# A transformer block on one NeuronCore: where the first group's mean and scale copy, and its first two q/k evictions, stand in the order of ScalarE and VectorE

## The chip, the core and the metric

The kernel runs on 1 core of one Trainium2 chip, as one launch. The metric is the device time of that core in microseconds (us); lower is better. All data are fp32 in memory. A large operand of a matmul is held as two parts, a rounded high part and the rest (`hi` and `lo`), and a product takes three matmuls (`hi*hi`, `hi*lo`, `lo*hi`) or, for some, two.

## The reference, cut to what matters

```python
x = x + _layernorm(attn(_layernorm(x), Wqkv, bqkv, Wo, bo))     # x: 1 x 2048 x 1024, head width d = 256
x = x + _layernorm(ffn(_layernorm(x), W_gate, W_up, W_down))    # F = 2752
# attn:
qkv = einsum('bsc,cf->bsf', x, Wqkv) + bqkv          # q, k, v: 2048 x 256 each
attn = softmax(einsum('bqd,bkd->bqk', q, k) / sqrt(d))
out = einsum('bqk,bkd->bqd', attn, v) @ Wo + bo
# ffn: silu(x @ W_gate.T) * (x @ W_up.T) @ W_down.T
```

The change lies in the first stage, the q, k and v of the normalised `x`. The kernel multiplies the raw `x` by the weights and puts the layer norm in afterwards: with the row mean m and the row scale r, (x - m) r W = r (x W - m sum(W)), so that each result needs m, r and the sums of the weights' columns when it leaves the accumulator bank.

## The kernel before, in words

**Tiles.** The 2048 rows are four groups (g = 0 to 3) of 512, each of four blocks (tb) of 128. PSUM has eight banks of 128 x 512 fp32. `bank[0]` to `bank[3]` take the four q/k results of a group (two halves of k, two of q, features on the partitions); `vb[0]` to `vb[3]` (banks 6, 7, 4, 5) take the four v blocks (rows on the partitions). The fp32 staging tiles (`f4`, `f2p`, `stage`, 4 KB a partition each) are used again and again, for columns of x, rows of x and weights.

**The steps of a group.**
- `x_parts` (L183 on ScalarE, L184 on VectorE) makes the high and the low part of the group's columns of x.
- `row_stats` (VectorE, L196 to L199) or `row_stats_scalar` (ScalarE L204 and L206, GpSimd L205 and L207 to L209) finds m and r of a block of rows.
- `store_mr` and `load_mr` (SP) write a group's m and r to memory and read them back broadcast over the partitions; `turn_mr` (L220, ScalarE) copies them into the order in which q/k need them.
- `qk` (L127 to L129, TensorE, 24 matmuls into one bank) and `v_block` (L245 and L246, 16 matmuls into one bank) do the products. In the first group the products of v are made by `v_part` instead, before q and k.
- `qk_out` evicts a q/k bank: L231 (VectorE) reads the bank, the means from `turn_mr`'s copy and one column of the weight sums `nws`; L232 (VectorE) multiplies by r; L235 (ScalarE) adds the bias and rounds to the high part; L236 (VectorE) makes the low part. After L231 the bank is free.
- `v_out` evicts a v bank: L250, L252 (not in the first group) and L253 on VectorE, the copy L254 on ScalarE, the rest L255 on VectorE. The staging `vst` has two halves, so block tb + 2 overwrites that of tb.
- `take_sum(i)` (L387, ScalarE) sums one fourth of the rows of the turned q/k weights `wqk_t`, loaded by `load_sum`, into column i of `nws`.

**Order.** In this stage nearly every operation is kept in the order in which the program text names it (`pin`), on each engine by itself; an engine works through its own list in order and waits on semaphores for the others. So the order of the text is the order of each engine's list. The DMAs of this stage are all issued by SP, in text order too. From the end of the stage on, the main loop over 16 blocks of scores (`scores`, `softmax`, `turn`, `attend`, `proj`) and then the feed-forward part are placed by a scheduler; only some of their operations are pinned.

The text around the change, before: after the fourth q/k product of group 0 come the four evictions of group 0's v blocks, each followed by one weight sum; then `turn_mr(0)`; then four loads; then the first two v blocks of group 1 with their evictions; then the q/k evictions of group 0, with the row statistics of group 1's last two blocks between them. TensorE's list at that place is: the four `qk(0, i)`, the four `v_block(1, tb)`, the four `qk(1, i)` into the same banks 0 to 3, the four `v_block(2, tb)`, and so on.

Of the kernel before, what the change touches and what calls it, by code (L numbers as in the profile page):

```python
# [24 lines left out]
TB = G // P  # L25
# [9 lines left out]
def block_kernel(ctx, tc, x, xt, wqk, wqk_t, wv, bqk, bv, wo, bo, wgu, wlast, wd, out):  # L35
# [17 lines left out]
    def tl(p, shape, dt, name):  # L53
        return p.tile(shape, dt, tag=name, name=name, bufs=1)
# [17 lines left out]
    def small_tile():  # L72
        small_n[0] += 1
        return small[small_n[0] % NSM]

    bank_pool = pool("banks", space=PSUM)
    bank = [tl(bank_pool, [P, 512], F32, f"bank{i}") for i in range(8)]
# [28 lines left out]
    def f32(ap):  # L106
        return ap.bitcast(F32)
# [27 lines left out]
    def kT(d, g):  # L135
        return slot(kx, 4 * d + g)
# [3 lines left out]
    def vt(k, h=slice(0, 2)):  # L140
        return (a1 if k < 8 else late_v[0]).rearrange("p a b c -> p (a b c)").rearrange("p (k h d) -> p k h d", h=2, d=D)[:, k % 8, h, :]
# [27 lines left out]
    def load(dst, src):  # L169
        pin(nc.sync.dma_start(dst, src))  # L170
# [5 lines left out]
    def load_row(g, tb):  # L176
        t = g * TB + tb
        load(row_room[g][tb], x[t * P : (t + 1) * P, :])

    def x_parts(g, c0, n, r):  # L180
        d = xT[g % 2][:, c0 : c0 + n, :, :]
        v = r[:, : n * G].rearrange("p (c t) -> p c t", c=n)
        pin(nc.scalar.copy(d[:, :, 0, :], v))  # L183
        pin(nc.vector.tensor_tensor(d[:, :, 1, :], v, f32(d[:, :, 0, :]), ALU.subtract))  # L184

    def m_of(g, tb):
        return yg[g][:, 2 * tb : 2 * tb + 1]

    def r_of(g, tb):
        return yg[g][:, 2 * tb + 1 : 2 * tb + 2]  # L190
# [10 lines left out]
    def row_stats_scalar(g, tb):  # L201

        s, r = small_tile(), row_room[g][tb]
        pin(nc.scalar.activation(r, r, AF.Identity, accum_out=s[:, 0:1]))  # L204
        pin(nc.gpsimd.tensor_scalar(s[:, 1:2], s[:, 0:1], -1.0 / C, None, ALU.mult))  # L205
        pin(nc.scalar.activation(r, r, AF.Square, bias=s[:, 1:2], accum_out=s[:, 2:3]))  # L206
        pin(nc.gpsimd.tensor_scalar(m_of(g, tb), s[:, 0:1], 1.0 / C, None, ALU.mult))  # L207
        pin(nc.gpsimd.tensor_scalar(s[:, 3:4], s[:, 2:3], 1.0 / C, EPS, ALU.mult, ALU.add))
        pin(nc.gpsimd.tensor_tensor(r_of(g, tb), s[:, 3:4], mhalf, ALU.pow))  # L209
# [8 lines left out]
    def turn_mr(g):  # L218

        pin(nc.scalar.copy(  # L220
            mr[g].rearrange("q (k b p) -> q k b p", k=2, b=TB), mr_raw[g].rearrange("q (p b k) -> q k b p", k=2, b=TB)
        ))
# [6 lines left out]
    def qk_out(g, i, b, pin=pin):  # L229
        s, bias = qst[i % 2], bqk_s[:, i : i + 1]  # L230
        pin(nc.vector.scalar_tensor_tensor(s, mr[g][:, L], nws[:, i : i + 1], b, ALU.mult, ALU.add))  # L231
        pin(nc.vector.tensor_tensor(s, s, mr[g][:, R], ALU.mult))  # L232
        if i < 2 or g == 0:
            dst = kT(i, g) if i < 2 else qa[:, i - 2, :, :]
            pin(nc.scalar.activation(dst[:, 0, :], s, AF.Identity, bias=bias))  # L235
            pin(nc.vector.scalar_tensor_tensor(dst[:, 1, :], s, bias, f32(dst[:, 0, :]), ALU.add, ALU.subtract))  # L236
        else:
            pin(nc.scalar.activation(s, s, AF.Identity, bias=bias))
            pin(nc.sync.dma_start(q_d[g][:, i - 2, :], s))

    def v_block(g, tb, b, pin=pin):
        xg = xT[g % 2]
        cols = slice(tb * P, (tb + 1) * P)
        for c in range(8):
            pin(nc.tensor.matmul(b, xg[:, c, 0, cols], wv_s[:, c, :, :].rearrange("p a f -> p (a f)"), start=(c == 0), stop=False))  # L245
            pin(nc.tensor.matmul(b[:, D:], xg[:, c, 1, cols], wv_s[:, c, 0, :], start=False, stop=(c == 7)))  # L246

    def v_out(g, tb, b, both=True, pin=pin):
        k, s = g * TB + tb, vst[tb % 2]
        pin(nc.vector.scalar_tensor_tensor(s, nwv, m_of(g, tb), b[:, :D], ALU.mult, ALU.add))  # L250
        if both:
            pin(nc.vector.tensor_tensor(s, b[:, D:], s, ALU.add))  # L252
        pin(nc.vector.scalar_tensor_tensor(s, s, r_of(g, tb), bv_s, ALU.mult, ALU.add))  # L253
        pin(nc.scalar.copy(vt(k, 0), s))  # L254
        pin(nc.vector.tensor_tensor(vt(k, 1), s, f32(vt(k, 0)), ALU.subtract))  # L255
# [25 lines left out]
    def hi(dst, src):  # L281
        pin(nc.scalar.copy(dst, src))
# [20 lines left out]
    vb = bank[6], bank[7], bank[4], bank[5]  # L303
# [82 lines left out]
    def take_sum(i):  # L386
        pin(nc.scalar.activation(col_room[1][i], col_room[1][i], AF.Identity, scale=-1.0, accum_out=nws[:, i : i + 1]))  # L387
# [13 lines left out]
        row_stats_scalar(1, tb)  # L401
        load_row(2, tb + 2)
    hi(nwv, vb[0][:, D:])
    for tb in range(TB):
        v_out(0, tb, vb[tb], False)
        take_sum(tb)
    load(bo_s, bo.partition_broadcast(P))


# [93 lines left out]

    cols = lambda g, n: load_cols(g, 2 * n, 2, col_room[g][n])
    parts = lambda g: [x_parts(g, 2 * n, 2, col_room[g][n]) for n in range(4)]
    turn_mr(0)
    cols(2, 0)
    cols(2, 1)
    load_row(2, 0)
    load_row(2, 1)  # L510
    for tb in range(2):
        v_block(1, tb, vb[tb])
        v_out(1, tb, vb[tb])
    qk_out(0, 0, bank[0])
    row_stats_scalar(1, 2)
    qk_out(0, 1, bank[1])
    row_stats_scalar(1, 3)
    cols(2, 2)
    cols(2, 3)
# [854 lines left out]
```

## Time and profile before

| What | Value |
|---|---|
| Time, median of 3 runs | 1664.43 us (1662.71, 1664.43, 1665.21) |
| The profiled execution's own time | 1662.63 us |
| Its span, first to last instruction | 1660.8 us |
| Around the span | 1.8 us |
| TensorE matmul busy in the span | 1648.2 us (99%) |
| VectorE / ScalarE / GpSimd busy | 1105.0 / 736.4 / 107.5 us |
| Mean granted TensorE clock | 0.999 |

The profile is of one execution, and its times are counted from the start of the span. "PE" is TensorE's matmuls, "PEld" its weight loads, "DVE" VectorE, "ACT" ScalarE, "POOL" GpSimd, and "SPq" the queue in which SP issues DMAs. L231 is line 231 of the kernel before. A row of the timeline gives start, duration, engine, line, operation and tiles, and in square brackets the engine's idle time ahead of it with what ended it. Idle time of an engine that does not set the end costs nothing. The staging tile of the v evictions appears as `f`, that of the q/k evictions as `f2p`, the bank's second operand as `ys` (statistics and weight sums).

### The profile page before, as it was taken

The numbers are of one execution on the slowest core, as the hardware profiler recorded it, in microseconds if no ns is written. First come the engines' busy times: TensorE is split into PE (matmuls) and PEld (weight loads), VectorE is DVE, ScalarE is ACT, GpSimd is POOL, SyncE is SP. The second block draws the span as 40 slices with busy tenths as digits, with TensorE's granted clock in tenths as the row PEclk, the third lists the DMA queues.
The fourth block names the chain that finished last, engine by engine and source line by source line (L and its number), as shares of the span: only waits on it lengthen the run. The fifth ranks groups of instructions, "written<-read, shape, count | busy, mean of one in ns | idle before, by whom it ended". The sixth has DMA issues, their size and how long they took to land.

```text
span 1660.8 us, 21107 instructions
## 1 busy us (share of the span) xinstructions
PE 1648.2 (99%) x7705; PEld 1375.0 (83%) x7705; DVE 1105.0 (67%) x1657; ACT 736.4 (44%) x1094; POOL 107.5 (6%) x157
## 2 busy tenths in 40 slices
PE   9999999999999999999999999999999999999998
PEld 8788888888888888888888888888888888888887
DVE  6656677668877777777587458965556665455458
ACT  5673555445544444444365344433333333354342
POOL 3020000000011111111000001100000000000001
PEclk9999999999999999999999999999999999999999
DMA  8452133435756666656468656533222233676653
GB/s 316 156 185 70 46 107 107 139 121 191 232 182 215 220 215 227 205 198 216 143 228 276 196 190 222 187 134 105 101 96 95 96 102 121 229 261 197 197 186 123
DMA packets 137545, 283.62 MB, mean 171 GB/s; under 512 B 14304, under 2 KB 31072, under 8 KB 137440
## 3 DMA queue, kind: packets, MB, share of 16 engines
q1 hardware_dynamic: 136288, 280.30, 50.4%
q10 hardware_dynamic: 1152, 1.97, 0.3%
q8 instruction: 60, 0.98, 0.2%
q14 instruction: 45, 0.37, 0.1%
HBM read 198.31 MB, written 83.90 MB: 170 GB/s over the span
## 4 chain that ended last, share of the span: by engine, by line
PE 95%; DMA 2%; DVE 1%; ACT 1%; issue 0%; SPq 0%; POOL 0%; POOLq 0%; DVEq 0%
PE bank L859 73%; PE bank L127 4%; PE bank L128 4%; PE bank L129 4%; PE bank L460 3%; PE bank L444 2%; PE bank L461 2%; PE bank L245 1%; PE bank L592 1%; DMA stage<-wqk 1%; DMA f<-xt 0%; PE bank L246 0%; DMA stage<-wqk_t 0%; PE bank L1045 0%; PE bank L1044 0%
## 5 line engine op out<-in xcount | busy, mean ns | idle before, releaser
L859 PE MATMUL bank<-a 128*128 128x512 f32 (+1 forms) x960 | 226.4, 386 | 0.0
L859 PE MATMUL bank<-xb,a 128*128 128x512 f32 x912 | 212.2, 389 | 0.0
L859 PEld LDWEIGHTS bank<-a 128*128 128x128 f32 x960 | 179.1, 188 | 36.6
L859 PEld LDWEIGHTS bank<-xb,a 128*128 128x128 f32 x912 | 171.0, 188 | 35.4
L110 ACT CAST a<-f2p 128x1024 fp32r<-128x1024 f32 (+2 forms) x123 | 107.0, 870 | 113.4 <-PE bank L859 86.1
L111 DVE TENSOR_TENSOR a<-f2p,a 128x1024 fp32r<-128x1024 f32 (+2 forms) x123 | 122.3, 995 | 45.5 <-ACT a L110 41.6
L111 DVE TENSOR_TENSOR a<-f,a 128x1024 fp32r<-128x1024 f32 (+1 forms) x70 | 78.6, 1122 | 102.7 <-ACT a L110 98.6
L859 PE MATMUL bank<-kx,a 128*128 128x512 f32 x612 | 146.0, 389 | 0.0
L859 PEld LDWEIGHTS bank<-kx,a 128*128 128x128 f32 x612 | 114.9, 188 | 23.8
L859 PE MATMUL bank<-wvo 128*128 128x512 f32 (+1 forms) x498 | 120.9, 386 | 0.0
L873 DVE TENSOR_TENSOR p_s<-bank,p_s 128x512 f32<-128x512 f32 x96 | 65.1, 681 | 79.5 <-PE bank L859 43.8
L859 PEld LDWEIGHTS bank<-wvo 128*128 128x128 f32 x498 | 92.9, 188 | 18.9
L110 ACT CAST a<-f 128x1024 fp32r<-128x1024 f32 (+1 forms) x70 | 57.8, 825 | 103.0 <-PE bank L859 98.5
L859 PE MATMUL bank<-kx,wvo 128*128 128x512 f32 x420 | 100.1, 389 | 0.0
L859 PE MATMUL bank<-a,a 128*128 128x512 f32 x420 | 99.4, 389 | 0.0
L859 PEld LDWEIGHTS bank<-kx,wvo 128*128 128x128 f32 x420 | 78.8, 188 | 16.4
L859 PEld LDWEIGHTS bank<-a,a 128*128 128x128 f32 x420 | 78.8, 188 | 16.4
L111 DVE TENSOR_TENSOR wvo<-f,wvo 128x1024 fp32r<-128x1024 f32 (+1 forms) x47 | 54.6, 1162 | 49.2 <-ACT wvo L110 49.2
L859 PE MATMUL bank<-a1b,wvo 128*128 128x512 f32 x360 | 86.6, 389 | 0.0
L859 PEld LDWEIGHTS bank<-a1b,wvo 128*128 128x128 f32 x360 | 67.6, 188 | 14.0
L859 PE MATMUL bank<-kx 128*128 128x512 f32 (+1 forms) x339 | 78.5, 387 | 0.0
L859 PEld LDWEIGHTS bank<-kx 128*128 128x128 f32 x339 | 63.4, 188 | 13.0
(329 smaller groups left out, 3078.5 us busy)
## 6 DMA issues: line engine op xcount, KB each, us to landing
f2p<-wgu SPq DMA_DIRECT2D x41, 512.0 KB, 5.5
hd_S<-p_s SPq DMA_DIRECT2D x60, 256.0 KB, 4.6
f<-x SPq DMA_DIRECT2D x28, 512.0 KB, 4.2
f<-wgu SPq DMA_DIRECT2D x22, 512.0 KB, 3.5
wr<-wgu SPq DMA_DIRECT2D x21, 512.0 KB, 5.5
f<-wd SPq DMA_DIRECT2D x20, 512.0 KB, 5.3
hd_A<-xi SPq DMA_DIRECT2D x40, 256.0 KB, 2.0
td_T<-f SPq DMA_DIRECT2D x40, 256.0 KB, 4.5
```

The lines of the kernel that those rows point to most:

```text
L110: nc.scalar.copy(hi, src)
L111: (lo_engine or nc.vector).tensor_tensor(lo, src, f32(hi), ALU.subtract)
L127: pin(nc.tensor.matmul(o, w[0], m[0], start=first, stop=False))
L128: pin(nc.tensor.matmul(o, w[0], m[1], start=False, stop=False))
L129: return pin(nc.tensor.matmul(o, w[1], m[0], start=False, stop=last))
L245: pin(nc.tensor.matmul(b, xg[:, c, 0, cols], wv_s[:, c, :, :].rearrange("p a f -> p (a f)"), start=(c == 0), stop=False))
L444: nc.tensor.transpose(b[:, n * P : (n + 1) * P], p_s[:, k * P : (k + 1) * P], ident)
L460: nc.tensor.matmul(b, p[:, k, 0, :], vt(k).rearrange("p h d -> p (h d)"), start=(k == 0), stop=False)
L461: nc.tensor.matmul(b[:, D:], p[:, k, 1, :], vt(k, 0), start=False, stop=(k == NKB - 1))
L592: nc.tensor.transpose(o[:, j * P : (j + 1) * P], a[:, cb * P : (cb + 1) * P], ident)
L859: one = nc.tensor.matmul(o, w[i], m[j], start=first and n == 0, stop=last and n == 2, skip_group_check=chained)
L873: nc.vector.tensor_tensor(o, a, b, op)
```

## The change

Two things move, and no instruction is added or taken away. The copy `turn_mr(0)` goes from behind the four v evictions and weight sums of group 0 to a place behind the first v eviction; the weight sums come one eviction later in the text than they did. The first q/k eviction of group 0, `qk_out(0, 0)`, goes ahead of the first two v blocks of group 1, and the second one, with the row statistics before it, goes between those two blocks' evictions.

```diff
@@ end of the first group @@
     hi(nwv, vb[0][:, D:])
-    for tb in range(TB):
+    v_out(0, 0, vb[0], False)
+    turn_mr(0)
+    for tb in range(1, TB):
         v_out(0, tb, vb[tb], False)
-        take_sum(tb)
+        take_sum(tb - 1)
+    take_sum(TB - 1)
     load(bo_s, bo.partition_broadcast(P))
@@ start of the second group @@
-    turn_mr(0)
     cols(2, 0)
     cols(2, 1)
     load_row(2, 0)
     load_row(2, 1)
+    qk_out(0, 0, bank[0])
     for tb in range(2):
         v_block(1, tb, vb[tb])
         v_out(1, tb, vb[tb])
-    qk_out(0, 0, bank[0])
-    row_stats_scalar(1, 2)
-    qk_out(0, 1, bank[1])
+        if tb == 0:
+            row_stats_scalar(1, 2)
+            qk_out(0, 1, bank[1])
     row_stats_scalar(1, 3)
     cols(2, 2)
     cols(2, 3)
```

In the built program TensorE's and GpSimd's lists are the same as before. ScalarE's and VectorE's differ only in the places of the moved operations. SP's list differs in one place, which the text does not name and the scheduler decided: near 110 us of the old span, the two loads of `wo` (L580), which stood behind the load of block 0's rows of x for the main loop (L1226), now stand ahead of it; the load of group 3's mean and scale follows all three as before.

## The prediction

> **What bounds the kernel now.** I read the page first, then TensorE's waits, then the timeline around the longest of them, then the chain of waits that leads into it. The page says that matmuls fill the span:
>
> ```profile
> PE 1648.2 (99%) x7705; PEld 1375.0 (83%) x7705; DVE 1105.0 (67%) x1657; ACT 736.4 (44%) x1094; POOL 107.5 (6%) x157
> ```
>
> So only TensorE's idle time can be won: 1660.8 - 1648.2 = 12.6 us in all. What TensorE waits for, over the whole span:
>
> ```profile
> PE bank L127 <- DVE f2p L231: 2.0, 1, 2.0
> PE bank L271 <- POOL ident masks.py:199: 1.4, 1, 1.4
> PE bank L310 <- ACT wvo L282: 0.8, 1, 0.8
> PE bank L460 <- ACT f2p L594: 0.6, 2, 0.3
> ```
>
> The longest wait happens once: the first matmul of `qk(1, 0)` waits until L231 of `qk_out(0, 0)` has read bank 0. The timeline there (TensorE, then ScalarE, then VectorE):
>
> ```profile
> 52.61 0.28 PE L246 MATMUL bank<-wvo,a 128*128 128x256 f32 x1
> 54.86 0.51 PE L127 MATMUL bank<-a,wqk 128*128 128x512 f32 x1 [1.97 <-DVE f2p L231]
> 55.20 0.39 PE L128 MATMUL bank<-a,wqk 128*128 128x512 f32 x1
> ...
> 39.69 0.41 ACT L254 CAST a<-f 128x256 fp32r<-128x256 f32 x1 [1.07 <-DVE f L253]
> 42.72 1.06 ACT L387 ACTIVATE stage<-stage 128x1024 f32<-128x1024 f32 x1 [2.62 <-DMA stage<-wqk_t]
> ...
> 48.81 2.23 ACT L220 COPY f2p<-f2p 128x1024 f32<-128x1024 f32 x1
> 50.96 0.40 ACT L254 CAST a<-f 128x256 fp32r<-128x256 f32 x1
> ...
> 54.06 0.74 DVE L231 SCALAR_TENSOR_TENSOR f2p<-f2p,ys,bank 128x512 f32<-128x512 f32 x1
> ```
>
> Bank 0 had been full since 25 us; its eviction ran at 54.06 because VectorE had two v evictions of group 1 ahead of it, and the first of these waited for L254 at 50.96, behind the 2.23 us copy L220. Meanwhile ScalarE had stood idle 2.62 us at 40.1, waiting for `wqk_t`. From the chain of waits for 30 to 56 us:
>
> ```profile
> 35.44 7.26 DMA stage<-wqk_t
> 42.72 1.15 ACT stage L387 x2
> ...
> 48.91 2.14 ACT f2p L220
> ```
>
> The wait is thus fed by a DMA, through ScalarE and VectorE in turns. Past it TensorE is solid: by stretches, PE is busy 21.74 of 21.80 us in 54.8 to 76.6, 63.40 of 63.40 in 76.6 to 140, 258.29 of 260 in 140 to 400, and 100.00 in each 100 us from 400 to 1600.
>
> **Part 1, the copy moves into ScalarE's hole.** The load of the mean and scale was issued at 34.58 and took 5.3 us, so it is there at 39.9; L254 of block 0 ends at 40.1. L220 then runs from 40.05 to 42.28 (2.23 us). The first `wqk_t` sum cannot start before 42.72 anyway, so the copy is free: what hides it is the 2.62 us DMA wait. If that cover were gone, it would cost ScalarE the 2.23 us that it costs now. L254 of block 1, which stood behind the first sum (43.77), goes to 42.2.
>
> **Part 2, the sums and the v evictions of group 0.** With 1.15 us for a sum, and per eviction 0.47 (L250), 0.48 (L253), 0.40 (L254), 0.43 (L255) and the trace's handovers of some 0.05: L254 of block 2 at 44.0, sum 1 at 44.3, L254 of block 3 at 45.9, L255 until 46.7, sums 2 and 3 from 46.2 to 48.3. The two later `wqk_t` loads (issued between 36.42 and 38.04, 8.8 us each) are in by 45.2 and 46.9; sums 2 and 3 start at 46.2 and 47.2, just in time. SP's queued loads of x behind the sums keep their times to 0.7 us; their readers are at 62.7 and later.
>
> **Part 3, the q/k evictions.** L231 of `qk_out(0, 0)` needs the copy (42.3), sum 0 (43.9) and VectorE (46.7): it runs 46.7 to 47.4 instead of 54.06 to 54.80. Then L232 to 48.1, L235 behind sum 3 until 49.0, L236 to 49.75. Behind that wait on VectorE is queued the v eviction of group 1's block 0 (L250 at 48.23 before, 49.7 now); nobody needs its bank until `v_block(2, 0)` at 76.7. By the same durations, with the row statistics at 1.25 + 0.35 + 1.25 us between, L231 of bank 1 ends at 52.7, of bank 2 at 58.7, of bank 3 at 63.7 (before: 65.63).
>
> **What TensorE gets.** It is through with `v_block(1, 3)` at 52.61 and would start L127 0.12 later (the step from L246 to the next matmul), at 52.73, the next at 52.96; that one ran at 55.20. The gain is 55.20 - 52.96 = 2.24 us. The Trainium skill (TensorE: Matmul & The Clock Gate, "What happens when you issue a matmul") says that weight loads are pulled ahead of matmuls; with the weights in already, the restart would be free and the gain 54.86 - 52.73 = 2.13. The trace disagrees: the weight load waited too, 2.3 us.
>
> **What is late next.** Banks 0 to 3 are wanted at 52.7, 58.2, 63.6 and 69.1 and free at 47.4, 52.7, 58.7 and 63.7: at least 4.9 us in hand each. Further on TensorE comes 2.24 us sooner, and VectorE and ScalarE 1.93 (63.7 against 65.63). The low part of group 2's last columns (L184, end 76.87) is read at 79.09, 2.22 in hand; that of group 3's first columns (end 108.2) at 110.08, 1.9 in hand. If the two engines did not move at all, TensorE would lose 2.24 - 1.9 = 0.4 there; with their 1.93, nothing. So the gain lies between 1.8 and 2.24. I take 2.24, as their chain runs without a pause that a DMA ends from 56 to 110 us. The rest of TensorE's waits (1.6 us from 180 us on) follow TensorE and stay.
>
> **Part 4, SP near 110 us.** The `wo` loads wait only for TensorE (110.04, just behind its last read), the row load for L184 (109.34). Swapped, the mean load behind them (111.02 before) still has the same three ahead: zero in the sum; the rival below prices it.
>
> Sum: span 1660.8 - 2.24 = 1658.6, own time 1662.63 - 2.24 = 1660.4. That execution lies 1.80 under the median; carried to the median, 1664.43 - 2.24 = **1662.2**, that is 0.13%. A measurement of this kernel can tell about 0.2% (3.3 us) from no change, so this is inside.
>
> **Rivals.**
>
> *The wait is longer in the other executions.* It hangs on a DMA, and the three runs spread by 2.5 us. If all of the 1.80 by which the median exceeds the profiled time sat in this wait, the median would win 2.24 + 1.80 = 4.04: 1660.4, 0.24% faster. For it: the chain's longest piece is a 7.26 us load. Against it: loads at the start, before 15 us, can vary too, and their share the change leaves. 20%.
>
> *The copy becomes the new wait.* In the trace L254 of block 1, whose input was there at 41.5, ran at 43.77, behind a sum that waited for a DMA. In the same way a late mean load now holds up three v evictions and four sums. (The Trainium skill, TensorE: Matmul & The Clock Gate, in its opening table, calls ScalarE's queue strictly first in, first out; the trace agrees with that 43.77.) ScalarE has 0.4 us to spare and bank 0 then 5.3, so nothing is lost unless the load lands after 45.8, 11.2 us from its issue, where it took 5.3 and the longest load in the first 120 us 10.5. Where it just eats the gain (48.0) the time is 1664.4. 5%, together with the case that scheduler and chip give no gain for another reason.
>
> *Slower: the mean load of group 3.* `turn_mr(3)` waited 3.4 us for it, until 117.15; L235 and L236 of k's second half queue behind and ended at 120.72; TensorE reads that low part at 124.36, 3.6 in hand. 2.24 sooner, it waits if the load lands after 118.5, the gain is gone at 120.8, and at 124.1 the kernel is 3.3 us slower (1667.7). Issued near 109.0 now, that is 15 us to landing, where it took 6.1 behind the same three loads. For it: the order on SP did change. 4%.
>
> *The change does not do what it says.* The built lists show the new places, and the copy's load stands ahead of `wqk_t`'s on SP; this leaves 1%: 1664.4.
>
> **How the numbers follow.** Forecast 70%, longer wait 20%, new wait or no gain 6%, slower 4%. The range: from the longer wait (1660.4, less 0.5 of run spread: 1659.9) to no gain (1664.4). The forecast's own range is 1660.9 to 1663.9: the gain of 1.8 to 2.24 with half the runs' spread, 1.25, on both sides. Faster by over 0.2% (below 1661.1): the longer wait, and a little of the forecast's lower edge, 0.22. Slower by over 0.2%: 0.04. Within: 0.74.
>
> **What would show it.** Right: L220 near 40 us, inside what was the 2.62 us idle; L231 of bank 0 near 46.7; no wait of L127 on L231 in TensorE's list; a span near 1658.6. Wrong: an idle TensorE in 50 to 70 us, a new wait near 77, 110 or 122, or a longer span with those waits gone, which would mean that the time is not TensorE's idle time at all.

## The result, and the profile after

The changed kernel takes 1660.77 us (median of 21 runs, 1659.82 to 1661.93) against 1663.36 us for the kernel before in the same comparison (21 runs, 1660.50 to 1667.06). The ratio is 0.9983 with a 95% interval of 0.9977 to 0.9990: 0.17% faster, clear of zero and inside the 0.2% that was called no change. The forecast was a gain of 2.24 us; the medians differ by 2.6, with 1.7 to 3.8 by the interval. The forecast time was 1662.2, 1.4 us above the measured one. The runs of after lie within 2.1 us of each other, those of before within 6.6.

The page of after, its first part: matmuls are busy for the same 1648 us, in a span that is 1.8 us shorter.

```profile
span 1659.0 us, 21108 instructions
...
PE 1648.4 (99%) x7705; PEld 1375.1 (83%) x7705; DVE 1104.7 (67%) x1657; ACT 736.0 (44%) x1094; POOL 108.1 (7%) x157
```

TensorE's waits over the whole span of after: the 2.0 us of L127 on L231 is gone, and what headed the list behind it now heads it, unchanged.

```profile
PE bank L271 <- POOL ident masks.py:199: 1.4, 1, 1.4
PE bank L310 <- ACT wvo L282: 0.9, 1, 0.9
PE bank L463 <- ACT f2p L597: 0.6, 2, 0.3
```

The timeline of after around the place, TensorE, then ScalarE, then VectorE (start, duration, then the row as before). The matmul of `qk(1, 0)` follows the last one of `v_block(1, 3)` 0.12 us after its start, the ordinary step. The copy L220 stands in the old hole, and the first sum finds its load there as soon as ScalarE is free. L231 reads bank 0 5.8 us before TensorE wants it.

```profile
52.88 0.28 PE L246 MATMUL bank<-wvo,a 128*128 128x256 f32 x1
53.00 0.40 PE L127 MATMUL bank<-a,wqk 128*128 128x512 f32 x1
53.24 0.40 PE L128 MATMUL bank<-a,wqk 128*128 128x512 f32 x1
...
40.34 0.41 ACT L254 CAST a<-f 128x256 fp32r<-128x256 f32 x1 [1.07 <-DVE f L253]
40.65 2.18 ACT L220 COPY f2p<-f2p 128x1024 f32<-128x1024 f32 x1
42.73 0.40 ACT L254 CAST a<-f 128x256 fp32r<-128x256 f32 x1
43.25 1.06 ACT L387 ACTIVATE stage<-stage 128x1024 f32<-128x1024 f32 x1
...
47.20 0.74 DVE L231 SCALAR_TENSOR_TENSOR f2p<-f2p,ys,bank 128x512 f32<-128x512 f32 x1
```

And the chain of waits for 30 to 56 us, which in before ran through the load of `wqk_t`, ScalarE and VectorE, is now TensorE alone:

```profile
by line: PE bank L245 28.8%; PE bank L127 19.4%; PE bank L129 19.2%; PE bank L128 18.4%; PE bank L246 14.6%; PE bank L395 0.9%
```

From the first matmul of `v_block(1, 0)` to the first of `qk(1, 0)` it is 53.00 - 41.71 = 11.29 us, where it was 54.86 - 41.44 = 13.42: 2.13 us. TensorE came to that stage 0.27 us later than in the profile of before, a difference that is there already at `qk(0, 0)` (19.66 against 19.39). 2.13 - 0.27 = 1.86 is what the spans differ by (1660.8 to 1659.0), so nothing of it is lost further on.

### The profile page after: what moved, and what is told of

The parts are those of the page before. It is cut to its first block, busy times and chain, and to the rows that moved or that the text cites. A ratio compares the mean times of both kernels' runs of the same rounds, so it can differ in the third digit from the quotient of the medians.

```text
span 1659.0 us, 21108 instructions
## 1 busy us (share of the span) xinstructions
PE 1648.4 (99%) x7705; PEld 1375.1 (83%) x7705; DVE 1104.7 (67%) x1657; ACT 736.0 (44%) x1094; POOL 108.1 (7%) x157
## 4 chain that ended last, share of the span: by engine, by line
PE 97%; DMA 1%; DVE 1%; issue 0%; ACT 0%; POOL 0%; POOLq 0%; SPq 0%; DVEq 0%
PE bank L862 72%; PE bank L127 4%; PE bank L129 4%; PE bank L128 4%; PE bank L463 3%; PE bank L464 2%; PE bank L447 2%; PE bank L245 1%; PE bank L310 1%; PE bank L246 1%; PE bank L595 1%; PE bank L1048 0%; PE bank L1047 0%; PE bank L459 0%; DMA f<-wv 0%
```

## The experiments

Two questions were open: which of the two moves brings the gain, and why the runs of before are spread so much wider than those of after.

### The copy moved alone

```diff
-    for tb in range(TB):
+    v_out(0, 0, vb[0], False)
+    turn_mr(0)
+    for tb in range(1, TB):
         v_out(0, tb, vb[tb], False)
-        take_sum(tb)
+        take_sum(tb - 1)
+    take_sum(TB - 1)
...
-    turn_mr(0)
     cols(2, 0)
```

TensorE's list is that of after, and SP's order near 110 us is that of before.

> The copy of the mean and scale moves into ScalarE's hole, the q/k evictions stay in the old order; the order of SP's loads near 110 us is the old one too. Theory A (the old wait of TensorE at L127 on L231 is fed by a DMA whose landing varies from execution to execution; it was 2.24 us in the profile of before, and by the spread of its runs from about 0 to 6.4 us): by the durations of the profile of after, VectorE reaches L231 of bank 0 at 51.95 behind both v evictions, the matmul would start at 52.75 and TensorE is there at 53.00, so the wait is gone with only 0.25 us in hand, and each execution's wait is 2.5 us shorter than before but not below zero. Median about 1661.0, lowest about 1660, highest about 1664.5. Theory B (the narrower spread of after comes from the swapped loads near 110 us, the wait is 2.24 in every execution): 2.24 off every run with the wide spread kept: median 1661.1, lowest near 1658.3, highest near 1664.8.

Measured: 1660.69 us (12 runs, 1659.73 to 1661.75), ratio 0.9981 (0.9973 to 0.9990) to a before of 1663.21. The timeline, ScalarE and VectorE:

```profile
39.53 2.21 ACT L220 COPY f2p<-f2p 128x1024 f32<-128x1024 f32 x1
41.64 0.40 ACT L254 CAST a<-f 128x256 fp32r<-128x256 f32 x1
41.94 1.06 ACT L387 ACTIVATE stage<-stage 128x1024 f32<-128x1024 f32 x1
...
50.83 0.74 DVE L231 SCALAR_TENSOR_TENSOR f2p<-f2p,ys,bank 128x512 f32<-128x512 f32 x1
```

TensorE started `qk(1, 0)` at 53.04 without a wait: L231 at 50.83, with the 0.80 to the matmul, is 1.4 us early. So the copy's move alone makes the whole gain, and the swapped loads near 110 us are worth nothing that these runs can tell, as the sum had it. The lowest runs are those of after and not 2 us under them, so theory B is out. The long tail that theory A asked for (to 1664.5) did not show either.

### The first eviction moved alone

```diff
+    qk_out(0, 0, bank[0])
     for tb in range(2):
         v_block(1, tb, vb[tb])
         v_out(1, tb, vb[tb])
-    qk_out(0, 0, bank[0])
     row_stats_scalar(1, 2)
```

> The kernel before with only the first q/k eviction ahead of the first two v blocks of group 1; the copy and the second eviction stay where they were. L231 of bank 0 runs behind the copy at 51.05, the matmul would start at 51.85 and TensorE is there at 52.73: no wait on bank 0 in an execution like the profile of before. But the two v evictions now stand between, and L231 of bank 1 moves from 56.99 to about 58.7; TensorE wants bank 1 at 58.17 and would start at 59.5. So the wait goes over to the next bank: 1.3 to 1.4 us there in place of 2.24. Theory A: 0.8 us under before, median 1662.5, spread as wide as before. Theory that the first eviction's place alone makes the gain: 1660.8, as after.

Measured: 1664.44 us (12 runs, 1661.24 to 1665.54), ratio 1.0002 (0.9993 to 1.0011): no gain, where 0.8 us was expected by theory A and the whole gain by the other. ScalarE and TensorE in its timeline:

```profile
49.77 2.21 ACT L220 COPY f2p<-f2p 128x1024 f32<-128x1024 f32 x1
...
60.41 0.50 PE L127 MATMUL bank<-a,wqk 128*128 128x512 f32 x1 [1.84 <-DVE f2p L231]
```

The wait went over to bank 1, as expected, with 1.84 us for the 1.3 to 1.4 reckoned; in this execution the first weight sum also started 0.96 us later than in the profile of before (43.68 against 42.72). What the expectation left out is the stretch of `v_block(2, tb)`: it took 88.95 - 76.89 = 12.06 us instead of 11.29, since ScalarE and VectorE came late to the columns of group 2. That is about the 0.8 us that should have been won. An eviction that is put earlier behind an unmoved producer does not help here; it pushes the next one back.

### One copy more, and five more, in the kernel after

```diff
     v_out(0, 0, vb[0], False)
-    turn_mr(0)
+    for _ in range(2):        # six in the second kernel
+        turn_mr(0)
```

> The kernel after with the copy of the mean and scale made twice in a row: 2.1 us more on ScalarE ahead of three v evictions and the four sums. In the profile of after, bank 0 is read at 47.2 and wanted at 53.0, bank of v block 2 is read (L250) by 43.98 and wanted at 47.35. Slack of 3.4 us at the v bank, 5.0 at bank 0: nothing lost, median 1660.8, no new wait of TensorE; at most a few tenths if late DMAs eat the slack in some executions. If the copy's time mattered one for one: 1662.9.

> The kernel after with the copy made six times in a row: 10.4 us more on ScalarE, 10.3 after the 0.1 us that it waited. Reading 1 (bank 0 is the first to be missed, as my prediction reckoned): L231 of bank 0 at 57.5, matmul at 58.3, wait 5.4, time 1666.2. Reading 2 (the v bank is missed first): L250 of block 2 at 53.8 to 54.3, TensorE stands at 47.35 for 6.9 us, bank 0 is then in time; time 1667.7. The weight-sum loads (in by 43.25 for the first) are now far ahead of need: if their late landing is what spread the runs of before, these runs lie within 2 us of each other although TensorE waits on the same chain; if the lateness comes from upstream (the load of the mean and scale or what feeds it), they spread by 5 us or more.

Two copies: 1662.01 us (12 runs), ratio 0.9989 (0.9980 to 0.9998), 1.24 over after. No bank was missed, but the expectation of no loss was wrong. TensorE and VectorE in its timeline:

```profile
76.90 0.39 PE L246 MATMUL bank<-wvo,xT 128*128 128x256 f32 x1 [0.45 <-DVE xT L184]
78.04 0.39 PE L246 MATMUL bank<-wvo,xT 128*128 128x256 f32 x1 [0.17 <-DVE xT L184]
...
75.62 2.36 DVE L184 TENSOR_TENSOR xT<-stage,xT 128x1024 fp32r<-128x1024 f32 x2 [0.53 <-ACT xT L183]
```

Those are the low parts of group 2's columns, the place that the prediction had named as late next. The stretch of `v_block(2, tb)` takes 12.29 us instead of 11.29, and that from `qk(3, 0)` to the first scores 11.25 instead of 10.88: 1.37 in all, for the 1.24 measured. So 2.2 us on ScalarE cost over half of themselves, more than 30 us later.

Six copies: 1669.57 us (6 runs, 1668.86 to 1671.07), ratio 1.0036 (1.0022 to 1.0049). Reading 2 holds: TensorE stands at the bank of v block 2, waiting for L250, not at bank 0. The runs lie within 2.2 us, which speaks for the weight-sum loads as what spread the runs of before, as far as six runs can. What was not foreseen is the pace behind it. TensorE's timeline, then two stretches (time on PE, PEld, DVE, ACT and POOL with counts, then the granted clock, the DMA share and GB/s):

```profile
53.39 0.80 PE L245 MATMUL bank<-wvo,a 128*128 128x512 f32 x1 [5.90 <-DVE f L250]
53.98 0.41 PE L246 MATMUL bank<-wvo,a 128*128 128x256 f32 x1
54.19 0.63 PE L245 MATMUL bank<-wvo,a 128*128 128x512 f32 x1
...
53.40:59.40 6.00, 6.00 (x19) 5.14 (x20) 4.03 (x8) 4.70 (x11) 0.00 (x0) 0.50 0.66 187
```

TensorE resumed 6.06 us late (47.33 would have been its turn, 0.12 behind the start of the last L246 at 47.21), and at half the clock until 59.4; a pair of L245 and L246 took 0.64 us instead of 0.352. Nine pairs in 5.92 us instead of 3.17 lose 2.75. 6.06 + 2.75 = 8.81; the medians differ by 8.80, the two profiled spans by 8.4 (1667.4 to 1659.0). The Trainium skill (TensorE: Matmul & The Clock Gate, "Part 1") has TensorE's clock halved after an idle window of about 3.4 us; the trace agrees for this 5.9 us, and in seven profiles a wait of 0.5 to 2.0 us at L127 did not do it.

### Other executions of the kernel before, and one without the weight-sum loads

Five more executions of before were profiled. 

> Another execution of the kernel before, unchanged, to see what its longer executions are made of. Since the copy moved alone kept all its runs within 2 us of each other, though by theory A a third of them should have shown a wait, theory A (the wait itself is up to 6 us long) is in doubt. Theory C: the wait is 0.5 to 3 us in every execution, and in some of them it also makes the TensorE clock drop for a while behind it, as behind the 5.9 us wait of the six copies (half speed for 6.8 us). By A the wait of L127 on L231 is the own time less 1660.8, whatever it is, at full clock. By C an execution up to 1663.5 looks so too, but one above 1665 shows a wait of 2 to 3 us and a stretch at half clock behind it, which makes up the rest.

The expectation of the second and third said the same in fewer words; that of the other two was:

> A further execution of before, in search of one above 1665: by theory A a wait of 5 us or more at full clock, by theory C a wait of 2 to 3 us with a half-clock stretch behind it; below 1664 the wait is the own time less 1660.8 by both.

The starts in this table are rows of each timeline; "late" is the distance from v block 0 to `qk(1, 0)` over the 11.29 us of after.

| Execution | First sum | Second sum | `v_block(1, 0)` | `qk(1, 0)` | Late | Own time |
|---|---|---|---|---|---|---|
| before, as shown ahead | 42.72 | 44.07 | 41.44 | 54.86 | 2.13 | 1662.63 |
| look 1 | 41.47 | 42.82 | 41.65 | 53.62 | 0.68 | 1661.52 |
| look 2 | 41.40 | 44.12 | 41.71 | 54.46 | 1.46 | 1662.51 |
| look 3 | 40.95 | 42.30 | 41.56 | 53.10 | 0.25 | 1661.82 |
| look 4 | 41.33 | 43.97 | 41.68 | 54.33 | 1.36 | 1661.79 |
| look 5 | 41.39 | 44.15 | 41.68 | 54.51 | 1.54 | 1661.96 |

All five are short executions at full clock, so they do not tell theory A from theory C. The own time less 1660.8, which both gave as the wait, comes within 0.8 us of the column "late" and no closer: the rest of an execution varies too.

Two of them, ScalarE and TensorE of the first look, then of the second:

```profile
41.47 1.06 ACT L387 ACTIVATE stage<-stage 128x1024 f32<-128x1024 f32 x1 [2.06 <-DMA stage<-wqk_t]
53.62 0.49 PE L127 MATMUL bank<-a,wqk 128*128 128x512 f32 x1 [0.52 <-DVE f2p L231]
```

```profile
41.40 1.06 ACT L387 ACTIVATE stage<-stage 128x1024 f32<-128x1024 f32 x1 [1.94 <-DMA stage<-wqk_t]
44.12 1.06 ACT L387 ACTIVATE stage<-stage 128x1024 f32<-128x1024 f32 x1 [1.27 <-DMA stage<-wqk_t]
54.46 0.50 PE L127 MATMUL bank<-a,wqk 128*128 128x512 f32 x1 [1.30 <-DVE f2p L231]
```

Where only the first sum waited for its load, the matmul came 12.14 or 12.15 us after that sum's start (42.72 to 54.86, 41.47 to 53.62, 40.95 to 53.10); where the second load was late too, it came 10.34 to 10.36 after the second sum's. The wait thus follows the later of two DMA landings, to a hundredth or two, and it differs from execution to execution. The profile on which the prediction rests had the longest wait of the six.

Part of that lies ahead of the load. SP issues in order, and ahead of `wqk_t` stands the load of the mean and scale (`f2p<-mr_d`), which waits until the small store of them (`mr_d<-ys`) has landed. SP's queue in the profile of before, then in the first look:

```profile
31.06 0.33 SPq L170 DMA_DIRECT2D mr_d<-ys  x1
34.58 0.33 SPq L170 DMA_DIRECT2D f2p<-mr_d  x1
35.44 0.90 SPq L170 DMA_DIRECT2D stage<-wqk_t  x2
```

```profile
31.42 0.33 SPq L170 DMA_DIRECT2D mr_d<-ys  x1
33.13 0.33 SPq L170 DMA_DIRECT2D f2p<-mr_d  x1
34.53 0.90 SPq L170 DMA_DIRECT2D stage<-wqk_t  x2
```

The store took 3.5 us to land in the profile of before and 1.7 in each of the five looks, and `wqk_t` was issued at 35.44 against 34.13 to 34.62. So 0.8 to 1.3 of the 1.2 to 1.8 us by which the first sum came later there are a late issue, and only the rest a slower load. In the profile of the first eviction moved alone the store took 3.9 us.

The other test of the same, with the loads left out:

```diff
     def load_sum(i):
-        load(col_room[1][i], wqk_t[i * P : (i + 1) * P, :])
+        pass
```

> The kernel before without the four loads of the turned q/k weights (2 MB); the weight sums are taken over what already lies in those tiles, so the sums are of other data. ScalarE's 2.62 us wait for the first load is gone, everything behind it comes 2.3 to 2.6 us sooner, and L231 of bank 0 (51.5 to 51.8) is just in time for TensorE at 52.73 with the 0.8 us to the matmul. If the wait's length is set by the landing of these loads: no wait or a few tenths, median 1660.8 to 1661.3, runs within 2 us. If by what lies upstream (the mean's load, the statistics): the median falls by 2 us at most and runs up to 1664 remain.

Measured: 1661.05 us (10 runs, 1660.63 to 1661.85), ratio 0.9983 (0.9973 to 0.9993). In the old order of the text, the wait is gone, as expected if these loads set it. Without the loads neither a late issue nor a slow load can hold the sums up, so this run does not tell those two apart.

```profile
39.16 1.06 ACT L387 ACTIVATE stage<-stage 128x1024 f32<-128x1024 f32 x1
...
52.51 0.40 PE L127 MATMUL bank<-a,wqk 128*128 128x512 f32 x1
```

### The copy doubled in the kernel before, and the copy moved alone once more

```diff
-    turn_mr(0)
+    for _ in range(2):
+        turn_mr(0)
     cols(2, 0)
```

> The kernel before with the copy of the mean and scale made twice, where it stood: all that leads to L231 of bank 0 comes 2.1 us later. Four executions of before showed waits of L127 on L231 of 0 to 2.0 us (the matmul 0.25, 0.7, 1.5 and 2.1 us late), with own times of 1661.8, 1661.5, 1662.5 and 1662.6, all at full clock; none reached the upper group of before's runs (1665 to 1667). Here the wait is 2.1 to 4.5 us. Theory A (the wait is all, one for one): median 2.1 over before, about 1664.7 to 1665.3, runs from 1662.8 to about 1666, with the upper group of before (where its wait would be 5 to 6) going to 1668 to 1669, that is two groups as in before, with the same shares. Theory C (a wait of some 2 us or more can drop the TensorE clock behind it, by the luck of where it falls): now most executions have it, the runs lie at 1666 to 1670, and the profile, if of such a run, shows a stretch at half clock behind the wait.

Measured: 1664.57 us (11 runs), ratio 1.0017 (1.0007 to 1.0026) to a before of 1662.39: 2.18 more, about the length of the copy. Nine runs lie at 1663.3 to 1666.0 and two at 1667.7 and 1669.3, so most did not go up as far as theory C asked. Its profile is of a run of 1663.32, with a wait of 1.7 us at full clock. The first sum started at 41.27 there and `qk(1, 0)` at 55.72, 14.45 us later where it was 12.15: one for one with the copy. The wait is no longer than that because TensorE itself came some 0.9 us late to the stage (the last section).

> The copy moved alone, once more, for its tail. Five looks at before gave waits up to 1.4 us at full clock and none of the executions above 1665, which were 6 of 29 beside the first runs of this kernel; the doubled copy in before's place raised the median by 2.2 us, one for one, and kept about the same share of long runs (2 of 11), so theory C (a wait of 2 us and more mostly drops the clock) is out as put. By theory A those long executions are late weight-sum loads with waits above 4.4 us; this kernel takes 2.45 us off the wait, so that some fifth of its runs should come in above 1662.7, two or three of a dozen, as none of the first dozen did. If again none does, theory A does not explain the long executions either, and what they are stays open. Median as before, 1660.7, the same as after to 0.05%.

Measured: 1661.00 us (12 runs, 1659.62 to 1662.85), ratio 0.9985 (0.9977 to 0.9994). One run of 24 in both sets is above 1662.7. Beside them 11 of 46 runs of before were above 1665, and by theory A as many of these runs, about 6 of 24, should have been above 1662.7. So waits that grow up to 6 us at full clock, one for one, do not account for before's longest runs. In this kernel's profile the first sum did wait 0.89 us for its load even behind the copy (until 43.50), L231 ran at 51.93, and TensorE started `qk(1, 0)` at 53.12 with 0.4 us in hand.

The mean granted clock, which is on record for each run, says more. In the twelve profiles that have the half clock only in the last 5 us of the span, the mean is 0.999 or 1.000; in that of the doubled copy, with one more stretch of 3.4 us at half clock, 0.998; in that of the six copies, with 6.8 us, 0.997. So a mean of 0.998 or less points to at least one such stretch.

| Runs | Number | With a mean clock of 0.998 or less |
|---|---|---|
| before, over 1665 us | 17 | 17 |
| before, the others | 57 | 15 |
| the copy doubled in before's place | 11 | 11 |
| after, the copy alone (twice), the loads left out | 55 | 5 |

The runs of before are the 74 that ran beside these experiments. Every long one thus held a stretch at half clock, as theory C has it and theory A does not. The stretch is not the whole of it: 3.4 us at half clock cost at most 1.7 us, and 6.8 us at most 3.4. With that taken off, the long runs were still 2.2 to 4.4 us above 1660.8; that is an estimate of their waits. The copy moved alone takes 2.45 us off a wait, which by the estimate leaves up to 2.0, or 1662.8; its 24 runs end at 1662.85. So the long runs fit a wait of 2 to 4 us with a stretch at half clock better than a wait of 6 us. Where the stretch lay in them, and whether the wait brought it on, is not shown: no long execution was caught in a profile, and in the one profile with 0.998 the stretch stood at the start of the kernel, while the wait of 1.7 us was followed by none. What is known besides: the long runs are absent where the wait is absent or has room (after, the copy alone, the loads left out).

## Why the prediction was right, point by point

**What bounds the kernel.** TensorE's idle time at one place, as read: its matmul time is 1648 us in both profiles, and the span fell by what left that place.

**Part 1, the copy in ScalarE's hole.** Right: L220 at 40.65 for 40.05, because ScalarE was 0.65 later there in that execution (L254 at 40.34 for 39.69), 2.18 us long, and the first sum started 0.12 after L254. The copy cost nothing, and moved alone it makes the whole gain.

**Parts 2 and 3, the evictions.** L231 of bank 0 at 47.20 for 46.7, most of the same 0.65 us. But the prediction did not ask what each part is worth: the evictions' move gives no time at all once the copy is moved, only room, 5.0 us at bank 0 (47.20 + 0.80 to 53.00) in place of 1.4. Without the copy's move the first of them just pushes the wait to bank 1.

**What TensorE gets.** 2.24 counted to the second matmul; measured in the same way (53.24 - 41.71 against 55.20 - 41.44) it is 2.23. In before the weight load had waited with its matmul, so the step to the second matmul was 0.34 us instead of 0.23 (54.86 to 55.20 against 52.73 to 52.96 in the sum), and that 0.11 was won too.

**What is late next.** The places were right, and that nothing is lost there: the low part of group 2's last columns ends at 75.46 in after and is read at 77.17, that of group 3's first ends near 106.7 and is read at 108.17. Two copies used this room up, and lost 1.37 us just there.

**Part 4, SP.** Zero, as summed, to what the runs can tell: with the old order of the three loads the copy alone takes the same time.

**The forecast for the median.** Here the step was weak, and that 2.24 and 2.6 lie so close is in part luck. The 2.24 us of one execution were carried to the median as if each had them; six profiled executions of before had 0.25 to 2.13. That the medians differ by 2.6 all the same comes in part from the long runs of before (9 of the 21 are above 1665 us), which the change removes and which the profile did not show. In the comparisons of the later experiments before's median was 1662.4 to 1663.2, 1.6 to 2.4 over 1660.77. The time itself was forecast 1.4 us too high: the median of three runs, 1664.43, lay 1.07 over that of 21, and the gain was 0.35 too small. So 1660.77 lies just under the forecast's own range of 1660.9 to 1663.9, and close to the 1660.4 of the rival "the wait is longer in the other executions". That rival was half right. The wait does vary with a DMA, and it was probably longer in the long runs. But in every execution that was profiled it was shorter, the rival put all of the excess down to the wait and nothing to the clock, and the chain's longest piece, the 7.26 us load, was not what mainly set the prediction's execution apart from the others: the 3.5 us store ahead of it was.

**The other rivals.** "The copy becomes the new wait" did not happen, and its point was set wrong: the first bank to be missed is that of v block 2, whose L250 in after ends at 43.98 and which TensorE wants at 47.35, 3.4 us, and not bank 0 with 5.3; the six copies showed it. And well before any bank, the columns of groups 2 and 3 begin to cost. "The mean load of group 3" did come later, in 6.6 us for 6.1:

```profile
116.23 2.15 ACT L220 COPY f<-f 128x1024 f32<-128x1024 f32 x1 [3.92 <-DMA f<-mr_d]
...
119.04 0.75 DVE L236 SCALAR_TENSOR_TENSOR kx<-f2p,bqk_s,kx 128x512 fp32r<-128x512 f32 x1 [4.56 <-ACT kx L235]
```

The low part is there at 119.79 and is read at 122.45: 2.7 us in hand where it was 3.6, so no wait.

## What to carry to other kernels

A copy that needs only an early load belongs into the hole in which its engine waits for a later load; look for such a hole upstream in the chain before moving the evictions downstream. Where a wait is fed by a DMA, its length in one profile is one draw: look at several executions before carrying it to the median, and expect the removal to narrow the spread as well. The room that a move leaves is the least over all the places that the delayed engine feeds, those 30 to 60 us later included, and not the room at the place that was repaired.

## What the runs showed of the hardware that was not expected

- In the six copies a 5.9 us wait of TensorE ended in a stretch of 6.8 us in which the granted clock was 0.50, some 0.8 us of it still within the wait; matmuls of 128x512 took 0.63 us instead of 0.40, and the wait cost 8.8 us instead of 6.1.
- In six executions of one kernel the landing of the same 0.5 MB load let the first sum start anywhere from 40.95 to 42.72 us, and the second started from 42.30 to 44.15. A small store ahead of these loads in SP's order landed after 1.7 us in five of them and after 3.5 us in the sixth, and moved the issue of all that stood behind it.
- In the profile of the doubled copy in before's place, the granted clock was at 0.50 from 7.6 to 11.0 us, right behind a wait of 1.9 us near the start (L310), and the stage that begins near 41.6 us elsewhere began at 42.59. In the six copies a wait of 1.7 us at that place was followed by no such stretch.

```profile
7.60:11.00 3.40, 3.40 (x17) 3.40 (x18) 2.34 (x4) 2.24 (x4) 0.00 (x0) 0.50 1.03 390
```
